# Chunk preparation in a fused attention block: token layout, order of the keys' turn, and who divides the entries' weights

## The chip, the core and the metric

One core of one Trainium2 chip. The metric is the device time of one launch in microseconds (us). The core's engines run side by side, each in the order of its own queue: TensorE (PE in the profile, its weight loads as PEld), VectorE (DVE), ScalarE (ACT), GpSimd (POOL), and SyncE (SP), which here issues nearly all DMAs, in order. Data meet between engines through semaphores.

## The reference

Four sequences of 1024 tokens, 512 features, 16 heads of 128. In short:

```python
xn = layernorm(x)
q  = rope(rmsnorm(xn @ Wq + bq, qn_w))                      # 16 heads
w  = softmax over each 4 tokens of (xn @ Wcmp + bcmp)
entries = sum over each 4 tokens of w * xn                  # 256 a sequence
ck = rope(rmsnorm(entries @ Wk + bk, kn_w), last position of the four)
cv = entries @ Wv + bv
sc = q . ck / sqrt(128), entries that end later masked; top 8 of them
ctx_sparse = softmax over the 8 chosen, times their cv
lk = rope(rmsnorm(xn @ Wlk + blk, kn_w)); lv = xn @ Wlv + blv
ctx_local  = softmax over the last 128 tokens and itself (q . lk / sqrt(128)) @ lv
attn = ((ctx_sparse + ctx_local) * 0.5) @ Wo + bo
ffn  = fp8(xn * scale) / scale  @  fp8(W2 * scale1) / scale1
out  = x + attn + ffn
```

## The kernel before

**Tiles and units.** The 4096 tokens are 32 chunks t of 128 tokens, eight a sequence; c = t mod 8. A unit is one chunk and two heads, so a chunk has eight units u = 0 to 7, and there are 256 units. All weights stay in SBUF. The main loop (L969) runs over a step s = 8t + u. It is a software pipeline written out by hand: step s does the scores, weighing and turning of unit s, the values of unit s - 1, the output of unit s - 2, the local values' projection of s + 1, the normalizing and rotating of the queries and keys of s + 2, and the projection of queries and keys of s + 3. The order of the calls in the loop's body is the order of instructions on every engine; no scheduler changes it.

**A unit on TensorE**, in its order: scores (L718, L725, L728), queries and keys (`queries`, L576, four 128x512 products), output (L921), local values (`values_of`, L682, four 128x256 products), values (`values`, L888). The fp32 products run as two matmuls each. `queries` and `values_of` have the turned tokens `xnT` (features on partitions) as the operand that is loaded as weights. `xnT` is a tile of 128 x 128 x 4: token, then block of 128 features, so `xnT[:, :, k]` steps by four floats. `xone` is a contiguous copy of block 0 with a row of ones in place of feature 0 (`put_ones`, L478 on ScalarE and L479 on GpSimd, at u = 3), which brings the biases in; it is made of `xnT`, which is fetched from DRAM at the end of u = 2 (`fetch_tokens`, L471, four DMAs).

**A unit on VectorE**: masks and row maxima of the window (L750), the entries' mask, their eight largest and their removal (L761 to L773); the normalizing of unit s + 2 (`normalize`, L604); `settle`: with ScalarE's exponentials (L775, L783) it drops the entries that were not chosen (L791), takes the reciprocals of both totals (L801) and divides the entries' weights (L803), while ScalarE divides the window's (`settle_window`, L811); the first half of the rotation (L327); `turn` (L829): 32x32 transposes of both heads' weights into `probB`.

**Turning through DRAM.** A full turn of 128 x 128 is done with VectorE's transposes within blocks of 32 and a write and a fetch that move the blocks. For the weights: one write `pr` (L837), four fetches `probT` (L871), which TensorE's `values` of the next step needs. For queries and keys of s + 2: the rest of the rotation (`end_rotation`, L329 and L330), `turn_keys` (L657 and L660, four writes `qk`, L665) and two fetches (`fetch_keys`, L675). On SP, in a step: `pr`, `qk`, `probT`, `qT` and `lkT`, with the preparation's DMAs between them. Chunk 0 and the last unit turn on TensorE (`turn_here`).

**Preparing a chunk** is a generator, `chunk_prep`, of which a step of the loop runs a piece or two: layer norm (L343 to L360, with a second mean by ScalarE's L352), the four tokens' softmax (L372 to L384, L399 to L401), the turning of the tokens within blocks (L392, into `xb`) and its write to DRAM (L397), the weighing (L403), the sum of each four (L411) and its write (L420). It starts at u = 7 and is driven by `steps()`, which runs twice a step: once after `turn`, once after `to_output`, both ahead of `end_rotation` and `turn_keys`. Chunks t + 4 are prepared in chunk t; in chunks 1 to 3 a second one (`extra`) goes along in u = 2 and 3. `chunk_entries` makes the compressed keys and values of a group of four chunks (PE L511, L541); `chunk_eight` makes the fp8 product (L558, in u = 5 and on; its additions on GpSimd), and its scratch tiles are the two buffers that `xb` uses too.

Of the kernel before, what the change touches and what calls it, by code (L numbers as in the profile page):

```python
# [38 lines left out]
def kernel(  # L39
# [299 lines left out]
    def chunk_prep(t):  # L339
# [6 lines left out]
        yield "A0"  # L346
        yield "B0"
# [11 lines left out]
        yield "A1"  # L359
        nc.vector.tensor_scalar(xt, xt, mean, r, ALU.subtract, ALU.mult)  # L360
        yield "B1"
        if not t:
            turn_tokens_here(xt)
            yield "T"
# [3 lines left out]
        xb = scratch(f"xb_{t}")  # L368
        log = work.tile([P, 1], F32, tag="log", name=f"log_{t}", bufs=1)
        row = work.tile([P, 2, BLK], F32, tag="row", name=f"row_{t}", bufs=1)  # L370
        red = work.tile([P, BLK // RATIO], F32, tag="red", name=f"red_{t}", bufs=1)
        nc.vector.scalar_tensor_tensor(  # L372
            xb, xt, 1.0, wcmp_sb, ALU.mult, ALU.mult, accum_out=log
        )
        nc.vector.tensor_scalar(row[:, 0, :], ones, log, bcmp_sb, ALU.mult, ALU.add)
# [9 lines left out]
        yield "A2"  # L385
        yield "B2"
        if not t:
            yield from add_tokens_here(row, red, xb, wide)
            return


        nc.vector.transpose(  # L392
            xb.rearrange("p (b j k) -> p b k j", b=NB, k=KK),
            xt.rearrange("p (k b i) -> p b k i", b=NB, k=KK),
        )
        tokens[t] = dram.tile([P, HID], F32, tag="xb", name=f"xb_dram_{t}", bufs=GC + 2)
        nc.sync.dma_start(tokens[t], xb)  # L397
        yield "A3"
# [3 lines left out]
        yield "B3"  # L402
        nc.vector.tensor_tensor(  # L403
            xt.rearrange("p (b j k) -> p b j k", b=NB, k=KK),
            xb.rearrange("p (b j k) -> p b j k", b=NB, k=KK),
            row[:, 1:2, :].unsqueeze(3).to_broadcast([P, NB, BLK, KK]),
            ALU.mult,
        )
        yield "A4"
        few = work.tile([P, P], F32, tag="few", name=f"few_{t}", bufs=1)  # L410
        nc.vector.tensor_reduce(  # L411
            few.rearrange("p (n k) -> p n k", k=KK),
            xt.rearrange("p (n r k) -> p n k r", r=RATIO, k=KK),
# [7 lines left out]
        yield "B4"  # L421

    def add_tokens_here(row, red, xb, wide):

        few = scratch("few_here")
        nc.gpsimd.memset(few, 0.0)
        fours = row[:, 1, :].rearrange("p (n r) -> p n r", r=RATIO)
        nc.vector.tensor_reduce(red, fours, AX.X, ALU.add)
        nc.vector.reciprocal(red, red)
        nc.vector.tensor_tensor(fours, fours, wide(red), ALU.mult)  # L430
        nc.vector.transpose(row[:, 0, :], row[:, 1, :])
        wp = pp("weights_here")
        nc.tensor.matmul(
            wp[:, 0:P], row[:, 0, 0:1].to_broadcast([P, P]), ident, start=True, stop=True
        )
        yield "W"
        nc.vector.tensor_tensor(
            xb.rearrange("p (s k) -> p s k", k=KK),
            chunks[0][0],
            wp[:, 0:P].unsqueeze(2).to_broadcast([P, P, KK]),  # L440
            ALU.mult,
        )
        nc.vector.tensor_reduce(
            few[:, 0 : NE * KK].rearrange("p (n k) -> p n k", k=KK),
            xb.rearrange("p (n r k) -> p n k r", r=RATIO, k=KK),
            AX.X,
            ALU.add,
        )
        few_here.append(few)
        few_here.append(dram.tile([P, P], F32, tag="few_here", name="few_dram", bufs=1))  # L450
        nc.sync.dma_start(few_here[1], few[:, 0 : NE * KK])
        yield "B4"
# [3 lines left out]
    def turn_tokens_here(xt):  # L456

        xp = pp("xp")
        for k in range(KK):
            nc.tensor.transpose(xp[:, ts(k, P)], xt[:, ts(k, P)], ident)  # L460
        xnT = work.tile([P, P, KK], F32, tag="xnT", name="xnT_0")
        nc.scalar.copy(
            xnT.rearrange("p s k -> p k s"), xp.rearrange("p (k s) -> p k s", k=KK)
        )
        chunks[0] = (xnT, None)

    def fetch_tokens(t):
        xnT = work.tile([P, P, KK], F32, tag="xnT", name=f"xnT_{t}")
        turned = tokens.pop(t).rearrange("(a i) (b x) -> b i a x", a=NB, b=NB)
        for b in range(NB):  # L470
            nc.sync.dma_start(  # L471
                xnT[ds(b * BLK, BLK)].rearrange("i (a j) k -> i a (j k)", a=NB), turned[b]
            )
        chunks[t] = (xnT, work.tile([P, P], F32, tag="xone", name=f"xone_{t}"))

    def put_ones(t):
        xnT, xone = chunks[t]
        nc.scalar.copy(xone, xnT[:, :, 0])  # L478
        nc.gpsimd.memset(xone[0:1], 1.0)  # L479

    def chunk_entries(g, n):
# [10 lines left out]
        else:  # L492
            few = scratch(f"fewT_{g}_{n}")
# [14 lines left out]
        yield "B4"  # L508
# [10 lines left out]
        kv = work.tile([P, 2, D], F32, tag="kv", name=f"kv_{g}_{n}", bufs=1)  # L519
# [26 lines left out]
    def chunk_eight(t):  # L546
# [4 lines left out]
        src = xnT.rearrange("p s k -> p (s k)")  # L551
# [3 lines left out]
        x8 = x8.rearrange("p (s k) -> p s k", k=KK)  # L555
        fp = pp(f"fp_{t}")
        for k in range(KK):
            nc.tensor.matmul(  # L558
                fp, x8[:, :, k], w2_sb[:, k, :], start=(k == 0), stop=(k == KK - 1)
            )  # L560
# [10 lines left out]
    def queries(n):  # L571
# [3 lines left out]
        for k in range(KK):  # L575
            nc.tensor.matmul(  # L576
                qp,
                xnT[:, :, k] if k or not t else xone,
# [98 lines left out]
    def values_of(n):  # L677
# [3 lines left out]
        for k in range(KK):  # L681
            nc.tensor.matmul(  # L682
                vp[:, 0:256],
                xnT[:, :, k],
# [101 lines left out]
    def settle(n):  # L786
# [15 lines left out]
        for h in range(2):  # L802
            nc.vector.tensor_scalar(  # L803
                probs[h][:, spa], probs[h][:, spa], tot[:, h, 1:2], None, ALU.mult
            )

    def settle_window(n):
        _, _, loc, _ = columns(n)
        tot = units[n].pop("tot")
        for h in range(2):  # L810
            nc.scalar.mul(probs[h][:, loc], probs[h][:, loc], tot[:, h, 0:1])  # L811
# [129 lines left out]
    def until(g, step):  # L941
        for at in g:
            if at == step:
                break
# [12 lines left out]

    ready = {-1: [0], 0: [1], 1: [2, 3], 2: [4, 5], 3: [6, 7]}
    ready.update({t: [t + GC] for t in range(GC, NT - GC)})
    made = {0: (0, 2), 1: (0, GC), 3: (1, GC)}  # L960
# [3 lines left out]
    until(first, "T")  # L964
    small_constants()
    masks()
    start = chunk_entries(0, 1)

    for s in range(-3, NN + 2):  # L969
        t, u = place(s)  # L970

        if u == 7 and t + 1 in ready:
            regular = chunk_prep(ready[t + 1][0])
            running.append(regular)
        if u == 3 and 0 <= t < NT:
            load_x(t, "sum")
        if u == 4 and t in made:
            running.append(chunk_entries(*made[t]))
# [11 lines left out]
        if s < 0:  # L990
            if s == -3:
                until(first, "B4")
# [4 lines left out]
        for_unit(s, (settle_window,))  # L997
        for_unit(s + 2, (go_on_rotating,))
        if by_dma(s):
            turn(s)  # L1000
        steps()
        if len(ready.get(t, ())) == 2 and u in (2, 3):
            if u == 2:
                extra = chunk_prep(ready[t][1])
            until(extra, "A0" if u == 2 else "A2")
            if u == 2:
                next(regular)
# [3 lines left out]
        if len(ready.get(t, ())) == 2 and u in (2, 3):  # L1011
            until(extra, "B1" if u == 2 else "B4")
        if len(ready.get(t, ())) == 2 and u == 1:
            next(regular)
        if u == 3 and 0 <= t < NT - 1:
            put_ones(t + 1)
        for_unit(s + 2, (end_rotation,))
        if s + 2 >= NU:
            for_unit(s + 2, (turn_keys,))
# [12 lines left out]
        if u == 1 and len(ready.get(t, ())) == 2:  # L1032
# [75 lines left out]
```

## Time and profile before

| what | us |
|---|---|
| three timed runs | 2717.34, 2717.20, 2714.86 |
| their median | 2717.2 |
| the profiled execution | 2725.9 |
| its span, first to last instruction | 2723.7 |
| TensorE busy in it | 2652.3 |
| VectorE, ScalarE, GpSimd busy | 2318.3, 1257.7, 799.1 |

Times of instructions come from the profiled execution, which took 8.7 us longer than the median. In a line of the timeline the columns are start, duration of the whole group, engine, line of the kernel, operation, out<-in, shapes and how many; in brackets the idle time before it and what ended it. Durations of neighbouring matmuls overlap, so what one costs is the distance from start to start. In a line of a tile, the three durations are the shortest, the median and the longest in ns, followed by the first and last start. A line of the stretches has the stretch, its length, and then for each engine its busy time and the number of instructions, TensorE's clock, the DMA engines' share and GB/s. The granted TensorE clock is 0.992 of full over the span.

### The profile page before, as it was taken

How to read it: one execution, taken by the hardware profiler on the slowest of the kernel's cores; microseconds unless marked ns; L12 is line 12 of the kernel's file. 1: busy time of each engine (PE TensorE's matmuls, PEld its weight loads, DVE VectorE, ACT ScalarE, POOL GpSimd, SP SyncE). 2: the span in 40 equal slices, each digit the busy share in tenths (PEclk: the TensorE clock that was granted, in tenths of full speed). 3: DMA queues.
4: the chain of work that ended last, by engine and by line, in shares of the span. 5: the costliest groups of instructions: out<-in, count | busy, mean ns of one | idle time of the engine just before them, and what ended most of it. 6: DMA issues, size and time to landing. Idle time of an engine off the chain costs nothing.

```text
span 2723.7 us, 46686 instructions
## 1 busy us (share of the span) xinstructions
PE 2652.3 (97%) x11802; PEld 2086.2 (77%) x11837; DVE 2318.3 (85%) x8884; ACT 1257.7 (46%) x5067; POOL 799.1 (29%) x1151
## 2 busy tenths in 40 slices
PE   8999999999999999999999999999999999999997
PEld 5777777777777777777777778777777777777776
DVE  7888888898888888888988888888988888888885
ACT  3444444444444444444444444444444444444443
POOL 4522332223332223232233322232323323222221
PEclk9999999999999999999999999999999999999998
DMA  8455455665545555566555555655665555566653
GB/s 257 120 142 150 132 149 167 171 165 153 154 135 158 151 157 149 161 166 169 160 145 139 155 151 154 170 159 157 168 164 146 150 141 147 151 161 165 162 153 107
DMA packets 667067, 422.85 MB, mean 155 GB/s; under 512 B 326528, under 2 KB 616112, under 8 KB 666800
## 3 DMA queue, kind: packets, MB, share of 16 engines
q1 hardware_dynamic: 666192, 419.46, 56.0%
q8 instruction: 97, 1.59, 0.3%
q14 instruction: 170, 1.39, 0.2%
q10 hardware_dynamic: 608, 0.41, 0.1%
HBM read 225.42 MB, written 194.25 MB: 154 GB/s over the span
## 4 chain that ended last, share of the span: by engine, by line
PE 76%; DVE 11%; DMA 5%; SPq 3%; ACT 3%; issue 2%; POOL 1%; DVEq 0%; ACTq 0%
PE qp L576 25%; PE vp L682 13%; PE cp L888 12%; PE op L921 12%; PE sc L728 5%; PE sc L725 4%; PE sc L718 3%; DMA probT<-pr 2%; SPq L665 1%; SPq L871 1%; ACT prob L775 1%; DVE probB L829 1%; DVE sc L750 1%; DVE taken L773 1%; PE fp L558 1%
## 5 line engine op out<-in xcount | busy, mean ns | idle before, releaser
L576 PE MATMUL qp<-wqk,xnT 128*128 128x512 f32 x1552 | 711.5, 595 | 3.5 <-DMA wqk<-in_L_attn_Wlk_dram 3.5
L576 PEld LDWEIGHTS qp<-wqk,xnT 128*128 128x128 f32 x1552 | 478.0, 309 | 221.4 <-issue 64.9
L775 ACT ACTIVATE prob<-sc,neg 128x256 f32<-128x256 f32 (+1 forms) x512 | 235.9, 461 | 879.2 <-DVE taken L773 861.1
L682 PEld LDWEIGHTS vp<-wlv,xnT 128*128 128x128 f32 x2048 | 517.8, 325 | 91.9 <-issue 56.2
L682 PE MATMUL vp<-wlv,xnT 128*128 128x256 f32 x2048 | 516.4, 395 | 0.1
L921 PE MATMUL op<-wo,cT 128*128 128x512 f32 x1024 | 481.6, 593 | 3.4 <-ACT cT L903 3.3
L325 POOL TENSOR_TENSOR rb<-th,cs 128x256 f32<-128x256 f32 x256 | 204.1, 797 | 949.7 <-DVE th L604 941.6
L750 DVE CUSTOM_DVE_ANT_0 sc<-sc,mask_b 128x256 f32<-128x256 f32 (+1 forms) x512 | 210.9, 412 | 180.8 <-PE sc L728 170.8
L811 ACT ACTIVATE prob<-prob,tot 128x256 f32<-128x256 f32 (+1 forms) x512 | 225.6, 488 | 300.3 <-DVE tot L801 297.6
L921 PEld LDWEIGHTS op<-wo,cT 128*128 128x128 f32 x1024 | 193.6, 190 | 206.8 <-issue 144.9
L888 PE MATMUL cp<-probT,lv 128*128 128x128 f32 x1920 | 307.0, 281 | 38.6 <-DMA probT<-pr 37.0
L888 PEld LDWEIGHTS cp<-probT,lv 128*128 128x128 f32 x1920 | 279.2, 197 | 55.8 <-issue 46.4
L311 ACT ACTIVATE junk<-qp 128x128 bf16<-128x128 f32 x1024 | 278.7, 272 | 30.6 <-PE qp L584 6.2
L604 DVE SCALAR_TENSOR_TENSOR th<-qp,r,norm_w 128x128 f32<-128x128 f32 x1024 | 286.2, 343 | 0.9 <-POOL r L306 0.9
L829 DVE STREAM_TRANSPOSE probB<-prob 128x512 f32<-128x512 f32 (+2 forms) x494 | 282.2, 609 | 0.1
L306 POOL TENSOR_TENSOR r<-r,nhalf 128x4 f32<-128x4 f32 x256 | 266.7, 1042 | 21.4
L305 POOL TENSOR_SCALAR r<-ss 128x4 f32<-128x4 f32 x256 | 61.6, 241 | 696.9 <-ACT junk L311 693.6
L791 DVE SCALAR_TENSOR_TENSOR prob<-taken,prob 128x128 f32<-128x128 bf16 (+7 forms) x512 | 182.8, 358 | 96.3 <-ACT prob L783 95.0
L888 PE MATMUL cp<-probT,cv 128*128 128x128 f32 x1536 | 259.9, 279 | 0.0
L576 PE MATMUL qp<-wqk,xone 128*128 128x512 f32 x496 | 258.5, 603 | 0.0
L728 PE MATMUL sc<-ckT,qT 128*128 128x96 f32 (+7 forms) x1024 | 228.2, 305 | 2.7 <-ACT ckT L543 2.7
L888 PEld LDWEIGHTS cp<-probT,cv 128*128 128x128 f32 x1536 | 217.3, 196 | 0.0
(143 smaller groups left out, 3844.9 us busy)
## 6 DMA issues: line engine op xcount, KB each, us to landing
pr<-probB SPq DMA_DIRECT2D x127, 512.0 KB, 3.3
probT<-pr SPq DMA_DIRECT2D x508, 128.0 KB, 3.0
qk<-thb SPq DMA_DIRECT2D x992, 64.0 KB, 1.8
pr<-probB SPq DMA_DIRECT2D x96, 384.0 KB, 2.3
probT<-pr SPq DMA_DIRECT2D x384, 96.0 KB, 2.5
qT<-qk SPq DMA_DIRECT2D x248, 128.0 KB, 2.9
lkT<-qk SPq DMA_DIRECT2D x248, 128.0 KB, 3.1
x_norm<-_attn_hidden_states_dram SPq DMA_DIRECT2D x32, 256.0 KB, 3.3
```

Source lines behind the costliest of these rows:

```text
L306: nc.gpsimd.tensor_tensor(r, r, nhalf[: ss.shape[0], 0:n], ALU.pow)
L311: nc.scalar.activation(junk[: src.shape[0]], src, AF.Square, accum_out=acc)
L576: nc.tensor.matmul(qp, xnT[:, :, k] if k or not t else xone, wqk_sb[u][:, k, :], start=(k == 0), stop=(t > 0 and k == KK - 1),)
L604: nc.vector.scalar_tensor_tensor(th[:, i, :], qp[:, ts(i, D)], r[:, i : i + 1], norm_w[:, i // 2, :], ALU.mult, ALU.mult,)
L682: nc.tensor.matmul(vp[:, 0:256], xnT[:, :, k], wlv_sb[u][:, k, :], start=(k == 0), stop=(k == KK - 1),)
L728: nc.tensor.matmul(sc[:, spa], q, ckT[:, 0:m], start=True, stop=True)
L750: nc.vector.tensor_tensor_reduce(sc[:, h, loc], sc[:, h, loc], mask_b[:, loc], -1.0, TAKEN, ALU.add, ALU.min, neg[h][0],)
L775: nc.scalar.activation(probs[h][:, loc], sc[:, h, loc], AF.Exp, bias=neg[h][0], scale=-1.0, accum_out=tot[:, h, 0:1],)
L811: nc.scalar.mul(probs[h][:, loc], probs[h][:, loc], tot[:, h, 0:1])
L829: nc.vector.transpose(pb[:, :, ds(h * g, g), :], prob[:, parts[0] * P : (parts[-1] + 1) * P].rearrange("p (g b i) -> p b g i", b=NB, i=BLK),)
L888: nc.tensor.matmul(blocks(cp[:, h, :]), v, probT[:, :, h * len(parts) + i - parts[0], :], start=(i == parts[0]), stop=(i == parts[-1]),)
L921: nc.tensor.matmul(op, cT[:, h, :], wo_sb[u][:, h, :], start=(u == 0 and h == 0), stop=(u == NU - 1 and h == 1),)
```

## The change

1. The turned tokens are laid out as 4 blocks x 128 tokens, so that `xnT[:, k, :]` is contiguous. VectorE's transpose writes runs of 32, the write to DRAM becomes four DMAs with runs of 32 floats, and the fetch takes whole rows of 512. The sum of fours reads contiguous fours and goes to the first quarter of `xb`. The scratch products of the logits, the entries' `fewT` and `kv` share one buffer.
2. `end_rotation` comes straight after the rotation's first half, and `turn_keys` straight after `turn`, both ahead of `steps()` and the preparation.
3. The preparation goes in named pieces at fixed places from u = 6 of the chunk before to u = 3, a second one from u = 2 to 5. `xone` is made at u = 4 instead of u = 3, in one buffer instead of two. Entries are begun (their loads) at the top of u = 4, and are made twice more, as `made` tells: of three chunks at t = 1 and t = 3.
4. ScalarE divides the entries' weights too, after the window's of the same head; VectorE no longer does.

```diff
@@ chunk_prep
-        yield "A0"
-        yield "B0"
+        yield "statistics"
...
+            xb = scratch(f"xb_{t}")
+            nc.vector.transpose(
+                xb.rearrange("p (b k j) -> p b k j", b=NB, k=KK),
+                xt.rearrange("p (k b i) -> p b k i", b=NB, k=KK),
+            )
+            tokens[t] = dram.tile(
+                [BLK, NB * KK, NB, BLK], F32, tag="xb", name=f"xb_dram_{t}", bufs=GC + 2
+            )
+            for a in range(NB):
+                nc.sync.dma_start(
+                    tokens[t].rearrange("i f a j -> a i f j")[a],
+                    xb[ds(a * BLK, BLK)].rearrange("i (f j) -> i f j", j=BLK),
+                )
...
+        yield "turned"
...
-            xb, xt, 1.0, wcmp_sb, ALU.mult, ALU.mult, accum_out=log
-        )
+            products, xt, 1.0, wcmp_sb, ALU.mult, ALU.mult, accum_out=log
+        )
+        yield "logits"
...
+        yield "exponentials"
...
-        nc.vector.transpose(
-            xb.rearrange("p (b j k) -> p b k j", b=NB, k=KK),
-            xt.rearrange("p (k b i) -> p b k i", b=NB, k=KK),
-        )
-        tokens[t] = dram.tile([P, HID], F32, tag="xb", name=f"xb_dram_{t}", bufs=GC + 2)
-        nc.sync.dma_start(tokens[t], xb)
...
-        few = work.tile([P, P], F32, tag="few", name=f"few_{t}", bufs=1)
+        few = xb[:, 0:P]
         nc.vector.tensor_reduce(
-            few.rearrange("p (n k) -> p n k", k=KK),
-            xt.rearrange("p (n r k) -> p n k r", r=RATIO, k=KK),
+            few.rearrange("p (b e k) -> p b k e", b=NB, k=KK),
+            xt.rearrange("p (b k e r) -> p b k e r", b=NB, k=KK, r=RATIO),
@@ fetch_tokens
-        xnT = work.tile([P, P, KK], F32, tag="xnT", name=f"xnT_{t}")
-        turned = tokens.pop(t).rearrange("(a i) (b x) -> b i a x", a=NB, b=NB)
+        xnT = work.tile([P, KK, P], F32, tag="xnT", name=f"xnT_{t}")
+        turned = tokens.pop(t).rearrange("i (b k) a j -> b i (k a j)", b=NB)
@@ put_ones
+        xone = work.tile([P, P], F32, tag="xone", name=f"xone_{t}", bufs=1)
@@ queries, values_of
-                xnT[:, :, k] if k or not t else xone,
+                xnT[:, k, :] if k or not t else xone,
...
-                xnT[:, :, k],
+                xnT[:, k, :],
@@ settle
-        for h in range(2):
-            nc.vector.tensor_scalar(
-                probs[h][:, spa], probs[h][:, spa], tot[:, h, 1:2], None, ALU.mult
-            )
-
-    def settle_window(n):
-        _, _, loc, _ = columns(n)
+
+    def divide(n):
+        _, _, loc, spa = columns(n)
         tot = units[n].pop("tot")
         for h in range(2):
-            nc.scalar.mul(probs[h][:, loc], probs[h][:, loc], tot[:, h, 0:1])
+            for part, cols in enumerate((loc, spa)):
+                nc.scalar.mul(probs[h][:, cols], probs[h][:, cols], tot[:, h, part : part + 1])
@@ the loop
+    FIRST_HALF = {6: "statistics", 7: "mean", 0: "logits", 1: "exponentials", 2: "weights", 3: "added"}
+    SECOND_HALF = {7: "turned", 2: "weighed"}
+    FIRST_HALF_MORE = {2: "statistics", 3: "normalized", 4: "weights", 5: "added"}
+    SECOND_HALF_MORE = {2: "mean", 3: "logits", 4: "weighed"}
...
-    made = {0: (0, 2), 1: (0, GC), 3: (1, GC)}
+    made = {0: (0, 2), 1: (0, 3), 2: (0, GC), 3: (1, 3), 4: (1, GC)}
...
         if u == 4 and t in made:
-            running.append(chunk_entries(*made[t]))
+            begun = chunk_entries(*made[t])
+            next(begun)
+        if u == 5 and t in made:
+            running.append(begun)
...
         for_unit(s, (settle,))
-        for_unit(s, (settle_window,))
-        for_unit(s + 2, (go_on_rotating,))
+        for_unit(s, (divide,))
+        for_unit(s + 2, (go_on_rotating,), (end_rotation,))
         if by_dma(s):
             turn(s)
+        if s + 2 >= NU:
+            for_unit(s + 2, (turn_keys,))
         steps()
...
+        host = t if u < 4 else t + 1
+        if host in ready:
+            until(regular, FIRST_HALF.get(u))
...
-        if u == 3 and 0 <= t < NT - 1:
+        if u == 4 and 0 <= t < NT - 1:
             put_ones(t + 1)
-        for_unit(s + 2, (end_rotation,))
-        if s + 2 >= NU:
-            for_unit(s + 2, (turn_keys,))
```

## The prediction

> **What bounds the kernel now.** I read the page first (busy shares, chain of work that ended last), then TensorE's waits, then the tiles that the change touches, then single units on the timeline. A unit is one pass of the loop: two heads of one 128-token chunk, eight units (u = 0 to 7) a chunk, 256 units. c is the chunk's place in its sequence.
>
> ```profile
> span 2723.7 us, 46686 instructions
> ...
> PE 2652.3 (97%) x11802; PEld 2086.2 (77%) x11837; DVE 2318.3 (85%) x8884; ACT 1257.7 (46%) x5067; POOL 799.1 (29%) x1151
> ...
> PE 76%; DVE 11%; DMA 5%; SPq 3%; ACT 3%; issue 2%; POOL 1%; DVEq 0%; ACTq 0%
> ```
>
> TensorE (PE) is busy 97% and is 76% of the chain, so 71.4 us are left in which it stands still, and apart from those the time is what its queue costs. VectorE (DVE) at 85% is next. TensorE's waits, in us in total, times, longest:
>
> ```profile
> PE cp L888 <- DMA probT<-pr: 37.0, 26, 4.0
> PE tp L852 <- ACT prob L811: 10.7, 4, 5.0
> ```
>
> 37.0 of the 71.4 us are waits for the turned probabilities, fetched from DRAM. By time, 5.9 of them lie in the last two units and 31 in chunks 1 to 30; these chunks have 39 us of TensorE waits in all (those over 0.15 us added up; the most of the rest are 4.1 for ckT and 2.8 for cT), the head and chunk 0 some 14, the tail 12. Two stretches of eight units, the second of the two without any preparation of a later chunk (columns: busy us of PE, its loads, VectorE, ScalarE, GpSimd):
>
> ```profile
> 1276.76:1364.50 87.74, 85.90 (x389) 68.00 (x389) 78.77 (x276) 39.93 (x156) 24.88 (x34) 1.00 0.59 160
> 2505.48:2590.14 84.66, 84.61 (x388) 67.64 (x389) 71.28 (x261) 38.95 (x153) 23.07 (x30) 1.00 0.59 159
> ```
>
> With preparation TensorE idles 1.8 us, without it nothing. So preparing chunks makes the waits, and the rest is matmul time.
>
> **Contiguous tokens: TensorE.** Weight loads and matmuls that read the turned tokens (min/median/max ns), and the load of the contiguous copy xone:
>
> ```profile
> L682 PEld LDWEIGHTS vp<-wlv,xnT x2048: 307/330/332, 27.3 to 2690.5; 128*128 128x128 f32 x187
> L682 PE MATMUL vp<-wlv,xnT x2048: 379/397/501, 27.5 to 2690.7; 128*128 128x256 f32 x187
> L576 PEld LDWEIGHTS qp<-wqk,xnT x1552: 307/308/333, 10.5 to 2668.3; 128*128 128x128 f32 x194
> ```
>
> ```profile
> L576 PEld LDWEIGHTS qp<-wqk,xone x496: 189/190/333, 88.8 to 2665.7; 128*128 128x128 f32 x166
> ```
>
> ```profile
> 1505.21 1.88 PE L921 MATMUL op<-wo,cT 128*128 128x512 f32 x4
> 1506.92 2.02 PE L682 MATMUL vp<-wlv,xnT 128*128 128x256 f32 x8
> 1508.78 0.61 PE L888 MATMUL cp<-probT,lv 128*128 128x128 f32 x4
> ```
>
> A load at a step of four floats takes 308 to 330 ns, a contiguous one 190. Under the 512-column matmuls this is hidden: four take 1506.92 - 1505.21 = 1.71 us, 428 ns each, with 190 ns loads, and the queries, with 308 ns loads, come at 428 ns too. The 256-column ones should take half, 214 ns, but eight take 1508.78 - 1506.92 = 1.86 us, 232 each. Contiguous loads therefore should give up to 8 x 18 = 0.15 us a unit; since some already run at the fastest duration I use mean 395 less min 379 over all 2048: **-32.8 us**. The bounds are 0 (the load is not what slows them) and 256 x 0.15 = 38. I take 32.8, because the contiguous loads of L888 keep up with 128-column matmuls at (0.61 - 0.28) / 3 = 0.11 us each.
>
> [...]
>
> The trace has 330 against 190 ns for the same 128 columns.
>
> **Added on TensorE.** Two more runs of the compressed entries, (0, 3) and (1, 3): eight matmuls of 232 ns and a transpose, 2.1 us each: **+4.2 us**. Nothing hides them.
>
> **VectorE.** A prepared chunk loses 1084 - 668 ns on the token transpose (L392 against the contiguous 128x512 ones of L829) and something of L411's 1063 (between none and 1063 - 652, the latter a plain pass of 512; I take 0.4): some 0.8 us a chunk. The sparse divide, 512 x 296 ns, goes to ScalarE. None of it is on TensorE's path; it buys room. But VectorE now waits for the divide before it turns the probabilities (queued behind: this transpose, the keys', the preparation, the next unit's weigh; the next waiting is SP with the write of pr). ScalarE does 256 + 192 columns twice, 0.44 and (estimated between the 0.30 and 0.44 of its neighbours) 0.37 us start to start, 1.6 us; VectorE meanwhile does the rotation (0.33 + 0.52) that is moved here and the first transpose. The second transpose ends about 0.3 us later than now at c = 6, 0.1 at c = 2.
>
> **Keys turned before the preparation.** Today, in a unit with preparation:
>
> ```profile
> 1987.11 0.34 SPq L837 DMA_DIRECT2D pr<-probB  x1
> 1989.32 0.36 SPq L931 DMA_DIRECT2D out_dram<-x_sum  x1
> 1990.53 2.61 SPq L665 DMA_DIRECT2D qk<-thb  x4
> 1993.25 1.83 SPq L871 DMA_DIRECT2D probT<-pr  x4
> ```
>
> SP is in order: the probT fetches stand behind the keys' four writes, and these wait until VectorE is through 1.6 us of preparation and x_sum's add. TensorE waited 1.71 us for this fetch at 1998.12. Afterwards the keys are turned 0.8 us after pr, so qk issues from 1987.9 and probT some 2.6 us earlier: this wait goes, and so do its like in u = 1 to 3. ScalarE's copy to xone, which today waits 33.8 us in all for the tokens' DMA and so delays cT, comes a unit later, and the 2.8 us of TensorE's waits for cT go as well.
>
> The entries' five loads now stand ahead of the unit's pr on SP, 2.2 us of issue. I set them to 0: SP is idle for over 4 us there (lkT issued by 2509.05, pr at 2513.43). Without that gap they would cost up to 2.2 us in twelve places. The tokens' fetch keeps its place and its four issues. The buffer that products, fewT and kv now share is taken at u = 0 and u = 4, after its last reader at u = 7 and u = 5: 0.
>
> **What is late next.** First, u = 7: the tokens' write becomes four DMAs instead of one, issued between the keys' writes and probT. In a unit without preparation at c = 6, probT's last issue starts at 2507.53 and TensorE gets to it at 2512.48; at 3.0 us to landing 1.95 us are spare. Four issues of 0.45 us, 0.3 for the divide, 0.15 for a faster TensorE and some 0.5 of traffic make 2.75: a wait of 0.8 us, less at c = 1 to 3 (2.5 us to landing). Over 31 chunks at 0.5 us: 15 us. How long 2048 pieces of 128 bytes take to write no row tells. Below: no delay (the fetches of 128-byte pieces, fewT<-pooled, land in 2.2 us, as the tokens' write does now). Above: the mean packet, 56.0% x 16 x 2723.7 us / 666192 = 36.6 ns, times 128 a DMA engine, 4.7 us. I stay by fewT.
>
> [...]
>
> Second, u = 5: xone is made one unit later, at u = 4, behind the four squares on ScalarE and behind the rstd on GpSimd, and the next unit's queries need it. At c = 2:
>
> ```profile
> 1506.55 0.18 DVE L801 RECIPROCAL tot<-tot 128x4 f32<-128x4 f32 x1
> ...
> 1506.83 0.91 ACT L811 ACTIVATE prob<-prob,tot 128x256 f32<-128x256 f32 x2 [0.91 <-DVE tot L801]
> ...
> 1509.55 1.01 POOL L306 TENSOR_TENSOR r<-r,nhalf 128x4 f32<-128x4 f32 x1
> ...
> 1511.47 1.08 PE L576 MATMUL qp<-wqk,xone 128*128 128x512 f32 x2
> ```
>
> Two more divides put the squares 0.55 us later, so rstd ends at 1511.1 and the 0.20 us memset at 1511.35; TensorE is there at 1511.47 - 0.12: no wait, and no room. At c = 7 weighing and divides are longer by more than the period is, and I get 0.95 us. Over eight chunks 2.5 us, over 31 **9.5 us**. All of TensorE's later work queues behind it.
>
> Chunk 0 and the head: two divides more before each tensor transpose (+0.3 us where TensorE waits), less preparation beside the weight folding; the tokens' write, moved a unit ahead, holds SP's weight loads some 4 us, which are needed 20 us later. I set it to 0, within 4 either way. Tail: +0.5.
>
> **The sum.** Matmul time -32.8 + 4.2 = -28.6. Waits of chunks 1 to 30: 39 now; 15 + 9.5 + 4 (entries, unchanged) afterwards: -10.5. Tail +0.5. In all -38.6. The profiled execution took 2725.9 us (span 2723.7 and 2.2 around it), so it would take 2687.3; the median of the three timed runs lies 8.7 lower: **2678 us**.
>
> **Rivals.**
> - All waits hide: the small pieces cost nothing and xone is in time, -24.5 more: 2654. For it: chunks without preparation wait for nothing. Against: both rooms worked out above are under 2 us.
> - The loads are not what slows the values' matmuls (nothing contiguous at 256 columns is in the trace): +32.8, 2711. The change would not do what its first words say. Against: 395 ns and 330 ns go together.
> - VectorE's wait for ScalarE and the full chain take the waits back: 20 us, 2698. For it: at c = 6 and 7 VectorE's busy time, 78.77 of 87.74 us, with its pauses is nearly TensorE's.
> - **Slower**: the small writes stand in the DMA engines ahead of probT at u = 7. At 4.7 us an engine, 2.8 are left when the last is issued, 2.3 more than I counted, 71 us over 31 chunks, of which some 7 fall into room left at c = 0 to 3: +64, 2742. It decides from 39 / 31 = 1.25 us a chunk more than I allow. For it: half the packets are small already and the engines are busy 56%. Against: fewT's 2.2 us.
>
> **Chances.** Forecast 0.45; all hidden 0.15; loads 0.08; waits taken back 0.16; slower 0.13; the rest, no change, 0.03. A measurement of this kernel tells about 0.2% (5.4 us) from no change. The loads' case ends near that line, so half of it counts as no change: faster 0.80, same 0.07, slower 0.13. The range goes from all hidden with 38 for the loads (2649) to the loads' case with its 4 us of the head (2715); it leaves out the slow case and a few.
>
> **What would show it.** Right: L682's loads at 190 and its matmuls at 379 ns; probT waits gone at u = 1 to 3 and left at u = 7; a new wait of qp for xone at u = 5, longest at c = 7. Wrong: matmuls still at 397 (step one); no waits left, or long probT waits at u = 7 with tokens' writes landing after 4 us (step two); VectorE waiting for ScalarE above 0.5 us a unit.

## The result and the profile after

The changed kernel took 2722.6 us (median of 20 runs, 2714.9 to 2730.5), the kernel before 2717.6 us (20 runs, 2714.3 to 2720.5). The ratio is 1.0016, 95% interval 1.0009 to 1.0023: no gain, and just measurably slower at most. The forecast was 2678. The profiled execution of the changed kernel took 2724.1 us, its span 2722.3, against 2725.9 and 2723.7 before, so the two profiles can be held side by side. They are not quite the medians: by the medians the changed kernel is 5.0 us slower, by the profiles 1.8 us faster, and what follows explains the profiles.

The page of the changed kernel (span, busy us and share of each engine, share of the chain that ended last):

```profile
span 2722.3 us, 46795 instructions
...
PE 2637.3 (97%) x11855; PEld 1796.1 (66%) x11855; DVE 2220.5 (82%) x8382; ACT 1397.7 (51%) x5587; POOL 795.2 (29%) x1159
...
PE 68%; DVE 13%; ACT 8%; DMA 4%; SPq 3%; issue 3%; POOL 2%; ACTq 0%; DVEq 0%; POOLq 0%
```

TensorE's busy time fell by 15.0 us and its idle time rose from 71.4 to 85.0. VectorE is 98 us lighter, yet the chain passes less through TensorE (68 for 76%) and more through ScalarE (8 for 3%). The values' loads and matmuls (ns shortest/median/longest):

```profile
L684 PEld LDWEIGHTS vp<-wlv,xnT x2048: 186/190/191, 28.6 to 2693.8; 128*128 128x128 f32 x187
L684 PE MATMUL vp<-wlv,xnT x2048: 378/379/390, 28.7 to 2694.0; 128*128 128x256 f32 x187
```

This is what was forecast, 190 and 379 ns for 330 and 397. Busy time of this group is 483.8 us for 516.4. So 32.6 us were gained here and lost again elsewhere. TensorE's waits say where (us in total, times, longest; L887, L851, L730 and L578 of this kernel stand at L888, L852, L728 and L576 in the kernel before):

```profile
PE cp L887 <- DMA probT<-pr: 30.1, 20, 3.6
PE sc L730 <- ACT ckT L545: 18.1, 10, 3.1
PE qp L578 <- POOL xone L481: 9.2, 12, 2.7
PE tp L851 <- ACT prob L810: 9.1, 3, 4.7
```

The sum for probT is little smaller than 37.0, but it is another wait. Before, the waits lay mostly at the values of units u = 1 to 3; of these 1.0 us is left. Now 17.5 us lie at u = 7 of chunks 4 to 26 (15 times; 1.7 of it is listed under "issue" and not under probT) and 10.1 at u = 3 of chunks 1 to 3: the units in which a chunk's tokens are written, the second in those chunks where two chunks are prepared. The ckT wait was 2.7 us before, at most 0.8 at a time. Here are SyncE's queue (SPq) and TensorE around one of the stalls at u = 7:

```profile
1133.84 0.34 SPq L836 DMA_DIRECT2D pr<-probB  x1
1134.49 2.86 SPq L667 DMA_DIRECT2D qk<-thb  x4
1137.44 2.57 SPq L374 DMA_DIRECT2D xb_dram<-xb  x4
1140.11 2.00 SPq L870 DMA_DIRECT2D probT<-pr  x4
```

```profile
1141.20 1.89 PE L684 MATMUL vp<-wlv,xnT 128*128 128x256 f32 x8
1145.03 0.68 PE L887 MATMUL cp<-probT,lv 128*128 128x128 f32 x4 [1.93 <-DMA probT<-pr]
```

The keys' writes now start 0.65 us after pr, as forecast, but the tokens' four writes hold SyncE for 2.57 us ahead of the probT fetch. All 124 of them:

```profile
L374 SPq DMA_DIRECT2D xb_dram<-xb x124: 549/626/1738, 33.2 to 2297.9; - x124
```

And what comes after such a stall, in three stretches of some 3.41 us (busy us of PE, its loads, VectorE, ScalarE, GpSimd, with their instructions, then TensorE's granted clock, the DMA share and GB/s):

```profile
1142.95:1146.36 3.41, 1.48 (x13) 1.36 (x13) 2.49 (x6) 1.20 (x8) 1.50 (x2) 1.00 1.15 280
1146.36:1149.78 3.42, 3.42 (x18) 3.42 (x17) 0.00 (x0) 1.00 (x3) 0.00 (x0) 0.50 0.52 154
1149.78:1153.19 3.41, 3.41 (x11) 1.74 (x11) 2.75 (x14) 0.00 (x0) 0.00 (x0) 1.00 0.77 147
```

The stall of 1.93 us is followed by 3.42 us at a granted clock of 0.50. In that stretch a pair of L720's matmuls takes 0.42 us from its start to the next pair's (at 1147.36), where it takes 0.24 at full clock (at 173.26). By an estimate, half the stretch, that is 1.7 us more of the same loss, and in the list of waits it is not seen at all. In the whole profile such half-clock time rose from 47.5 to 62.4 us (the last stretch of each runs on past the last instruction; within the spans it is 45.1 and 61.4).

### The profile page after: what moved, and what is told of

It is laid out like the page before. It is cut to its first block, busy times and chain, and to the rows that moved or that the text cites. A ratio compares the mean times of both kernels' runs of the same rounds, so it can differ in the third digit from the quotient of the medians.

```text
span 2722.3 us, 46795 instructions
## 1 busy us (share of the span) xinstructions
PE 2637.3 (97%) x11855; PEld 1796.1 (66%) x11855; DVE 2220.5 (82%) x8382; ACT 1397.7 (51%) x5587; POOL 795.2 (29%) x1159
## 2 busy tenths in 40 slices
DMA packets 719292, 423.33 MB, mean 156 GB/s; under 512 B 394496, under 2 KB 668336, under 8 KB 719024
## 4 chain that ended last, share of the span: by engine, by line
PE 68%; DVE 13%; ACT 8%; DMA 4%; SPq 3%; issue 3%; POOL 2%; ACTq 0%; DVEq 0%; POOLq 0%
PE qp L578 23%; PE op L920 11%; PE cp L887 11%; PE vp L684 11%; PE sc L730 4%; PE sc L727 3%; PE sc L720 3%; ACT prob L810 2%; ACT prob L777 2%; DMA probT<-pr 2%; DVE sc L752 2%; ACT junk L311 1%; DVE taken L775 1%; SPq L870 1%; ACT prob L785 1%
## 5 line engine op out<-in xcount | busy, mean ns | idle before, releaser
L578 PE MATMUL qp<-wqk,xnT 128*128 128x512 f32 x1552 | 720.4, 601 | 3.7 <-DMA wqk<-in_L_attn_Wlk_dram 3.7
L578 PEld LDWEIGHTS qp<-wqk,xnT 128*128 128x128 f32 x1552 | 300.0, 194 | 380.6 <-issue 379.4
L810 ACT ACTIVATE prob<-prob,tot 128x256 f32<-128x256 f32 (+7 forms) x1024 | 381.9, 443 | 298.4 <-DVE tot L803 298.4
L684 PEld LDWEIGHTS vp<-wlv,xnT 128*128 128x128 f32 x2048 | 389.4, 190 | 161.1 <-issue 116.0
L684 PE MATMUL vp<-wlv,xnT 128*128 128x256 f32 x2048 | 483.8, 379 | 0.0
L887 PE MATMUL cp<-probT,lv 128*128 128x128 f32 x1920 | 301.5, 277 | 32.3 <-DMA probT<-pr 30.1
L828 DVE STREAM_TRANSPOSE probB<-prob 128x512 f32<-128x512 f32 (+2 forms) x494 | 308.8, 630 | 12.4 <-ACT prob L810 1.2
L887 PEld LDWEIGHTS cp<-probT,lv 128*128 128x128 f32 x1920 | 273.7, 193 | 54.6 <-issue 42.9
L578 PE MATMUL qp<-wqk,xone 128*128 128x512 f32 x496 | 264.2, 615 | 9.8 <-POOL xone L481 9.2
L306 POOL TENSOR_TENSOR r<-r,nhalf 128x4 f32<-128x4 f32 x256 | 265.4, 1037 | 21.3
L887 PE MATMUL cp<-probT,cv 128*128 128x128 f32 x1536 | 257.8, 277 | 0.0
L730 PE MATMUL sc<-ckT,qT 128*128 128x96 f32 (+7 forms) x1024 | 229.5, 306 | 18.1 <-ACT ckT L545 18.1
L887 PEld LDWEIGHTS cp<-probT,cv 128*128 128x128 f32 x1536 | 215.1, 194 | 0.0
```

Source lines behind the costliest of these rows:

```text
L306: nc.gpsimd.tensor_tensor(r, r, nhalf[: ss.shape[0], 0:n], ALU.pow)
L578: nc.tensor.matmul(qp, xnT[:, k, :] if k or not t else xone, wqk_sb[u][:, k, :], start=(k == 0), stop=(t > 0 and k == KK - 1),)
L684: nc.tensor.matmul(vp[:, 0:256], xnT[:, k, :], wlv_sb[u][:, k, :], start=(k == 0), stop=(k == KK - 1),)
L730: nc.tensor.matmul(sc[:, spa], q, ckT[:, 0:m], start=True, stop=True)
L810: nc.scalar.mul(probs[h][:, cols], probs[h][:, cols], tot[:, h, part : part + 1])
L828: nc.vector.transpose(pb[:, :, ds(h * g, g), :], prob[:, parts[0] * P : (parts[-1] + 1) * P].rearrange("p (g b i) -> p b g i", b=NB, i=BLK),)
```

## The experiments

Theory A: the loads' gain is real, and it is given back by places in in-order queues: the tokens' writes ahead of probT on SyncE, the ckT copy and the ones behind other work on ScalarE and GpSimd, each wait made dearer by the clock. Rivals: B, the small pieces in the DMA engines; C, VectorE's chain or the divides on ScalarE; others where they are named. All kernels were timed beside the kernel before, and each ratio is against it. A difference to the changed kernel is one of medians from two such timings; in them the kernel before took 2717.3 to 2718.6 us.

**The layout alone.** The kernel before, with the contiguous tile, in two forms. First with one write of whole rows, which leaves out the regrouping of the four blocks of tokens (their order in the tile is not the reference's, the work of the engines is the same):

```diff
-                xnT[:, :, k],
+                xnT[:, k, :],
...
-            nc.sync.dma_start(
-                xnT[ds(b * BLK, BLK)].rearrange("i (a j) k -> i a (j k)", a=NB), turned[b]
-            )
+            nc.sync.dma_start(xnT[ds(b * BLK, BLK)], turned[b])
```

> The kernel before with the contiguous layout of the turned tokens alone, with its single write of 2 KB rows at its old place; as in the kernel with one write the regrouping of the four token blocks is left out. Nothing else of the change: keys turned where they were, preparation in its old stages, VectorE dividing the entries' weights. Theory A (the faster loads are worth their 32.6 us where no wait comes in their place): 24 to 36 us less than the kernel before, 2682 to 2694, with the 379 ns matmuls of vp and the 37.0 us of probT waits grown by less than 8. Rival C (VectorE's chain sets the pace there, so that a faster TensorE only waits longer): less than 12 us gained, 2705 to 2718, the waits for probT grown by 20 or more.

2689.2 us, ratio 0.9896 (0.9883 to 0.9910). Rival C falls: the gain of the loads reaches the end almost whole.

```profile
PE cp L884 <- DMA probT<-pr: 35.0, 26, 4.1
PE tp L848 <- ACT prob L807: 11.4, 4, 5.0
```

The waits are those of the kernel before. Then with the regrouping, in the true order of tokens, with the change's four writes at the old place of the one:

> The kernel before with the contiguous layout alone, with the change's four writes of 128-byte pieces at the old place of its single write (output in the reference's order). Theory A (each of the four issues takes 0.6 us of SyncE ahead of the fetch of probT): 15 to 45 us more than the 2689 of the same kernel with one write, 2704 to 2734, and probT waits of 50 to 80 us in place of 35.0. Rival F (the writes only hurt at u=7, where the change put them; at the old place they are covered): within 8 us of 2689.

2723.3 us, ratio 1.0021 (1.0012 to 1.0030): 34.1 us more than with one write, more than the whole gain.

```profile
PE cp L892 <- DMA probT<-pr: 55.5, 46, 5.6
```

So the writes are not dear at u = 7 only (F falls), but also at this second place ahead of a probT fetch; here the new waits lie at the values of u = 2 and u = 1.

**The keys ahead alone**, in the kernel before:

```diff
-        for_unit(s + 2, (go_on_rotating,))
+        for_unit(s + 2, (go_on_rotating,), (end_rotation,))
         if by_dma(s):
             turn(s)
+        if s + 2 >= NU:
+            for_unit(s + 2, (turn_keys,))
```

> The kernel before with the keys' turning alone moved ahead of the chunks' preparation (the rotation's end and the keys' transposes and DMA issues right behind the turning of the weights). Theory A (VectorE's order sets the probT waits at u=1 to u=3 only through the preparation that stands behind, not through the keys): small, minus 8 to plus 6 us against the kernel before, 2709 to 2724. Rival D (the keys moved ahead are themselves what costs: their four DMA issues now stand ahead of the fetch of probT on SyncE in every unit): slower by 8 to 25 us, with new waits for probT. The changed kernel shows 2.1 to 2.9 us for these issues where the kernel before shows 1.8.

2716.7 us, ratio 0.9995 (0.9986 to 1.0004). D falls, and the time is as A has it, but not for A's reason: the waits did change.

```profile
PE ep L511 <- DMA fewT<-pooled: 15.5, 8, 3.0
PE op L921 <- ACT cT L903: 11.8, 7, 2.4
PE cp L888 <- DMA probT<-pr: 11.3, 8, 3.2
```

The probT waits fell from 37.0 to 11.3 us; what came late instead is the preparation, whose sums TensorE now waits for at the entries. That keys ahead need a preparation that is begun earlier fits this, and fits the last kernels below, but was not run by itself.

**The tokens' writes**, in the changed kernel. The late write:

```diff
-            for a in range(NB):
-                nc.sync.dma_start(
...
+            unwritten.append((t, xb))
...
         if s + 2 >= NU:
             for_unit(s + 2, (fetch_keys,))
+        write_tokens()
```

> The changed kernel with the four DMA issues of a chunk's turned tokens kept back until after the fetch of the keys, so that on SyncE's queue they stand behind the fetch of probT instead of ahead of it. Theory A (the gain of the loads was given back to waits: the four issues take 2.6 us of SyncE at u=7, probT's fetch goes out late, TensorE waits at the product of values, and after each wait of about 2 us its granted clock is halved for some 3.4 us): the 30.1 us of waits of the context matmul for probT fall below 8, the half-clock time falls with them, 25 to 35 us less than the changed kernel, about 2690 to 2697. Rival B (not the issues, but the 2048 pieces of 128 bytes in the DMA engines delay probT): the pieces move later but still meet a transfer, the waits stay within 8 of 30.1, time within 6 us of the changed kernel. Rival C (TensorE waits for the VectorE chain, and SyncE is only the last to arrive): the waits change name, not size; time within 6 us.

2699.2 us, ratio 0.9938 (0.9926 to 0.9951), 23.4 less than the changed kernel, just short of the range of A.

```profile
PE qp L585 <- POOL xone L488: 20.9, 13, 6.2
PE sc L737 <- ACT ckT L552: 18.2, 10, 3.1
PE tp L858 <- ACT prob L817: 11.0, 4, 5.2
PE cp L894 <- DMA probT<-pr: 7.2, 6, 3.3
```

The waits for probT went. In chunks 1 to 3 the time was not kept: TensorE now waits there for the ones, 17.5 us at the next chunk's first queries where it was 6.0. The same writes issued by GpSimd (`nc.sync` to `nc.gpsimd` in that call, nothing else):

> The changed kernel with the four writes of the turned tokens issued by GpSimd in place of SyncE, at the same place of the program, with the same pieces of 128 bytes. Theory A (the time of SyncE's issues is what delays the fetch of probT): the probT waits at u=7 go as with the late write, to below 10 us, 12 to 25 us less than the changed kernel, 2698 to 2711; less of it if GpSimd's own issues delay the ones or the rotation. Rival B (the pieces in the DMA engines, ahead of probT's): the pieces still run at the same time, the waits stay above 25 us, time within 5 us of the changed kernel.

2697.9 us, ratio 0.9926 (0.9914 to 0.9939), probT waits 7.4 us. So these writes cost the probT fetch nothing once SyncE does not issue them. This run does not separate A from B, though: in its profile the pieces of 128 bytes are gone too. The packets under 512 bytes are 331008 where the changed kernel has 394496, fewer by 31 x 2048, and the writes stand on a queue of their own, half of whose packets are of 4096 bytes and half of 4:

```profile
q0 software_dynamic: 3968, 8.13, 1.1%
```

The changed kernel's own trace separates them. In chunks with c = 4 to 7, where the tokens' writes stand between, the last probT fetch is issued 6.98 us after pr (median of 12 units), elsewhere 4.18 us after it (115 units). From its issue to its landing it takes 3.21 and 3.11 us. So it is issued 2.8 us late, and the pieces ahead of it add 0.1 us: B falls by this. Last, whole rows from SyncE at the changed kernel's place, again without the regrouping, in one write and in four:

> The changed kernel with one write of whole 2 KB rows at the same place, and the reads as the kernel before has them (pieces of 512 bytes), into the contiguous tile; it leaves out the regrouping of the four blocks of tokens, so that their order in the tile is not the reference's, at the same work on every engine. Theory A (time of SyncE's issues): one issue of about 0.35 us in place of four of together 2.6 us, so about 2.2 us of lateness goes at each u=7: most of the 30.1 us of probT waits go, 18 to 32 us less than the changed kernel, 2691 to 2704. Rival B (pieces of 128 bytes in the engines): the same gain, but then the kernel with the late write gains nothing. Rival C (the VectorE chain): within 6 us.

> As the kernel with one write (whole 2 KB rows, regrouping left out), but in four writes of 32 rows at the same place. It tells the number of issues from the size of the pieces. Theory A with a price for each issue: four issues of about 0.4 us (the four of the keys took 1.8 us together), 1.3 us more than one write, so half of the probT waits are back: 6 to 14 us over the 2702 of the kernel with one write. Theory A with a price by pieces: an issue of 32 pieces is cheap, within 5 us of 2702. Rival B: within 5 us of 2702 as well, but then the writes by GpSimd gain nothing.

2702.0 (ratio 0.9944, 0.9932 to 0.9956) and 2702.4 us (0.9948, 0.9935 to 0.9961). The number of issues alone costs no time that can be told:

```profile
L372 SPq DMA_DIRECT2D xb_dram<-xb x124: 302/422/1579, 34.4 to 2281.2; - x124
```

An issue of 32 rows takes 0.42 us, one of 512 pieces 0.63. Four make 1.7 or 2.5 us, and the room before TensorE asks for probT, 1.95 us by the prediction's own reading, lies between; that this is why four issues of rows cost nothing is argued, not shown. In the profile of the four the probT waits are 16.8 us for 9.8, so the room is nearly used up.

**The ckT copy.** A dropped `yield "A7"` puts it right behind its transpose, ahead of the mean and the squares. In the changed kernel ScalarE is busy like this while TensorE waits 2.89 us for L545 at 738.48:

```profile
734.41 1.71 ACT L810 ACTIVATE prob<-prob,tot 128x256 f32<-128x256 f32 x4 [1.97 <-DVE tot L803]
736.02 0.71 ACT L351 ACTIVATE x_norm<-x_norm,off 128x512 f32<-128x512 f32 x1
...
736.73 0.25 ACT L311 ACTIVATE junk<-qp 128x128 bf16<-128x128 f32 x1
...
738.17 0.26 ACT L545 COPY ckT<-cp 128x128 f32<-128x128 f32 x1
```

Before, the divides of this unit took 0.91 us, and no mean stood between them and the squares:

```profile
735.52 0.91 ACT L811 ACTIVATE prob<-prob,tot 128x256 f32<-128x256 f32 x2 [1.97 <-DVE tot L801]
...
737.78 0.26 ACT L543 COPY ckT<-cp 128x128 f32<-128x128 f32 x1
```

The copy comes 3.76 us after the first divide's start instead of 2.26.

> The changed kernel with the copy of the entries' turned keys (ckT) put out right behind their transpose, one stage earlier in ScalarE's order, ahead of the mean's accumulation and the squares. Theory A (the copy is late because it stands behind what the change put ahead of it in ScalarE's queue): the 18.1 us of waits of the scores for ckT and the 1.9 us of the weights' transposes fall below 4, and the clock's halving behind the longest of them goes; 14 to 24 us less than the changed kernel, 2698 to 2708. Rival E (the copy is late because the entries' chain on VectorE and TensorE is late, whatever stands ahead on ScalarE): the waits stay within 5 of 18.1, time within 5 us.

2708.7 us, ratio 0.9967 (0.9955 to 0.9980), 13.9 less, just short of the range of A. The waits for ckT fell to 2.4 us (E falls), but those for probT rose:

```profile
PE cp L886 <- DMA probT<-pr: 41.7, 26, 3.2
```

TensorE comes to the values of u = 7 right after these scores, now up to 2.9 us earlier, and waits there instead.

**VectorE divides again** (the loop over `part` in `divide` cut to the window, and VectorE's `tensor_scalar` for the entries back):

> The changed kernel with VectorE dividing the entries' weights again, as the kernel before does; all else as changed. Theory A (the two more divides on ScalarE cost little of their own; the waits come from where the writes, the copy and the ones stand): within 8 us of the changed kernel, waits for ckT still above 12 and for probT above 25. Rival C (the divides on ScalarE are what made ckT, the ones and the weights late): the waits for ckT and the ones fall below 8 together, 15 to 30 us less than the changed kernel, 2692 to 2708.

2727.9 us, ratio 1.0035 (1.0021 to 1.0048), 5.3 more, at the edge of what can be told, with 15.4 us of waits for ckT and 39.0 for probT. The divides on ScalarE are no loss (a gain of 7.7 us in the kernel with all three places, below), and only a small part of ckT's lateness.

**The ones.** ScalarE's copy and GpSimd's row ahead of the preparation at u = 4:

```diff
+        if u == 4 and 0 <= t < NT - 1:
+            put_ones(t + 1)
         for_unit(s + 2, (go_on_rotating,), (end_rotation,))
```

(and the two lines gone from behind it). Alone, and then the other two without it:

> The changed kernel with the ones alone moved ahead of the chunks' preparation at u=4. Theory A (each wait has its own place and price): the 9.2 us of waits of the queries for the ones go, 5 to 12 us less than the changed kernel, 2710 to 2717. Rival H (TensorE's waits stand in series: a wait removed uncovers the next one in the same chunk): the waits for the ones go, but those for probT and ckT grow by about as much, within 4 us of the changed kernel.

> The changed kernel with the late write and the early ckT copy, the ones where the change put them. Theory A (the gains add): 23 and 14 us, 2685, and the ones are then worth some 22 us, since their waits grew to 20.9 us once the write was late. Rival H (in series): more than the sum, 2672 to 2680, because each of the two alone had its gain eaten by the other's wait (probT's waits rose from 30.1 to 41.7 us when ckT was early), and the ones are worth 10 to 15.

2715.8 us alone (0.9994, 0.9985 to 1.0003), 6.8 less than the changed kernel; its 9.2 us of waits went, and ckT's rose to 23.9. The time is as A has it, the growth elsewhere as H has it in part. The late write with the early copy: 2677.7 us (0.9856, 0.9842 to 0.9869), 44.9 less, where the two alone add up to 37.3. That is H's range: the waits stand in series, and each of the three repairs alone has the waits of another grow (the ones' from 9.2 to 20.9 us, probT's from 30.1 to 41.7, ckT's from 18.1 to 23.9).

**All three places.**

> The changed kernel with three places moved: the tokens' writes behind the fetch of the keys, the ckT copy right behind its transpose, and the ones (ScalarE's copy and GpSimd's row) ahead of the chunks' preparation at u=4 in place of behind it. Theory A (the waits are independent, each from a place in an in-order queue): the gains add, 23 from the writes, 14 to 24 from ckT, and 15 to 25 from the ones, whose wait had grown to 20.9 in the kernel with the late write: 2650 to 2675, and the half-clock time below that of the kernel before. Rival C (the chain of VectorE sets the pace and the next wait takes their place): 2690 to 2700, with new waits of the same sum elsewhere.

2662.6 us, ratio **0.9796** (0.9782 to 0.9809): 60.0 less than the changed kernel and 55 less than the one before.

```profile
PE tp L857 <- ACT prob L816: 9.7, 4, 4.7
PE cp L893 <- DMA probT<-pr: 8.5, 12, 2.3
PE cp L893 <- ACT cv L532: 5.5, 2, 2.8
PE sc L736 <- ACT ckT L551: 4.4, 5, 1.8
```

Half-clock time is 33.0 us. The singles add up to 44.1 (23.4, 13.9, 6.8), so 16 us come only together. Two parts of the change were then undone in this kernel:

> The kernel with the three places moved (2662.6), with the keys' turning put back behind the chunks' preparation, as the kernel before has it. Theory A (the keys ahead are what took away the probT waits of u=1 to u=3, 13 us at u=2 of chunks 8 to 27 and 20 us at u=3 of chunks 1 to 3 in the unit table): 10 to 30 us more than 2662.6, 2673 to 2693, with probT waits of 20 to 40 us. Rival G (the spreading over ten units is enough for that, the keys ahead are idle): within 6 us of 2662.6.

> The kernel with the three places moved (2662.6), with VectorE dividing the entries' weights again. In the changed kernel the same undoing cost 5 us. Theory A (VectorE's 65 us of work are off the path in most units, but late in those that host a chunk's preparation): 3 to 12 us more than 2662.6. Rival C (the divides on ScalarE hold up what stands behind them there): 3 or more us less.

With the keys behind the preparation 2716.6 us (0.9992, 0.9983 to 1.0001): 54.1 us more. The sign was A's, the size nearly twice what was expected. With VectorE dividing, 2670.2 us (0.9824, 0.9811 to 0.9838): 7.7 more. The first, on SyncE and TensorE:

```profile
1131.39 0.34 SPq L842 DMA_DIRECT2D pr<-probB  x1
1134.14 1.78 SPq L673 DMA_DIRECT2D qk<-thb  x4
1136.04 1.82 SPq L876 DMA_DIRECT2D probT<-pr  x4
```

```profile
PE cp L893 <- DMA probT<-pr: 51.2, 50, 4.3
```

The keys' writes go out 2.75 us after pr instead of 0.65, and the fetch behind them as late. With the preparation spread over ten units that happens in all of them, 50 waits for 26.

## Why the prediction was wrong

| term of the sum (us of the profile) | predicted | measured |
|---|---|---|
| contiguous loads | -32.8 | -32.6 |
| two more runs of the entries | +4.2 | +3.9 |
| old probT waits of chunks 1 to 30 | -31 | -31, with 1.0 left |
| probT behind the tokens' writes | +15 | +27.6 |
| the ones at u = 5 | +9.5 | +9.2 |
| ckT, against 4.1 before | 0 | +15.9 |
| cT | -2.8 | -1.9 |
| half clock, half of 62.4 - 47.5 (an estimate) | not counted | +7.4 |

The measured column adds up to -1.5 where the spans differ by -1.4. That is closer than it deserves: the tail, with some 6 us less in the last chunk, and small waits are not in it, the estimate for half clock counts stretches in which TensorE stands still too (6.7 us before, 5.1 in the changed kernel), and TensorE's busy time fell by 15.0 where the three terms that lie on it give 21.3.

- **Loads, keys, entries:** right in mechanism and size. For the loads the trace of the kernel before had 330 against 190 ns for the same 128 columns, the changed kernel has 190, and the layout alone, 28 us faster, shows that the gain reaches the time. The keys' step is also shown the other way round, by the 54 us that it costs to take it back. For **xone** the wait came where it was forecast in the unit, but its size is in part luck: 9.5 us were spread over 31 chunks, longest at c = 7 (0.95 us), and 6.0 of the 9.2 lie in chunks 1 to 3 (up to 2.7 us), where two chunks are prepared; at c = 7 it is 0.42.
- **The step that failed first** is "Four issues of 0.45 us ... Over 31 chunks at 0.5 us: 15 us". The mechanism and the place were named, and 15 became 27.6. Most of the lack is the second preparation of chunks 1 to 3, whose writes fall at u = 3 and were not counted there: 10.1 us in three stalls. The rest is at u = 7, 17.5 us: 0.45 us is about what an issue of the probT fetches or of the keys' writes takes (medians 0.43 and 0.45 us in the changed kernel), and one of 512 pieces takes 0.63 us. The question that was argued at length, how long the pieces take in the DMA engines, was the wrong one: behind them the fetch lands 3.21 us after its issue instead of 3.11. The slower rival (2742) falls with that; the estimate behind it took 36.6 ns a packet, and packets of 128 bytes took 11 ns (median in the changed kernel's trace).
- **"4 (entries, unchanged)"** is the second, and the larger error in the sum: the added divides were weighed for the probabilities and for the ones, but neither they nor the mean, now at u = 7, for the third thing that waits in ScalarE's queue, the ckT copy. Its waits measured 20.0 us (18.1 for the scores, 1.9 for a transpose), and moving it gave 13.9 us.
- **The clock** was not in the sum. It adds some 7.4 us net, by the estimate above.
- **The rival "waits taken back"** came true in its direction only: 20 us was its price, 37 were lost, and not through VectorE waiting for the divide. VectorE waits for that 1.2 us in the whole run, and taking the divide back made the kernel no faster. The loads' rival fell at once with 379 ns.

What stays open: how ckT's lateness divides between the mean, the divides and a TensorE that arrives earlier. Taking the divides away left 15.4 of the 18.1 us; the mean was not moved alone.

## What to carry to other kernels

For each instruction that a change adds or moves, list everything that stands behind it on its in-order engine and ask when each is due, and give a DMA issue the price of its own pattern: the same bytes took 0.34 us to issue as one write, 1.7 as four of whole rows and 2.5 as four in short runs. Give a place to what is due first (here the probT fetch, the ckT copy, the ones) ahead of work that is needed a chunk later. Test repairs together as well as alone, since waits that stand in series hide each other: 44 us by single repairs, 60 by all three.

## What the runs showed of the hardware

**The granted clock, in windows of 3.41 us.** In every profile here the half-clock stretches last 3.41 us or twice that (but for the one in which the profile ends) and begin on one grid of 3.41 us from start to end of the run. For the first ten profiles I added up TensorE's idle time in each grid window that itself had the full clock, from 100 us after the start to 60 us before the end. All 50 windows with 1.95 us or more idle were followed by half clock; of 20 with 1.7 to 1.95 us it was 8; of 7302 below 1.7 us none. In the six profiles taken afterwards, 30 of 30 windows above 1.9 us were followed by half clock, and none of 4376 below. The last 60 us, not in these counts, are less clean: 42 of 45 windows above 1.9 us were followed by half clock, and three, with 1.91, 1.97 and 2.00 us, were not. A stall's price went with where it fell. A stall of 3.33 us at 171.9 us of the changed kernel was cut by the grid into 1.63 and 1.70 and cost no clock, while one of 1.93 us inside a window cost the 1.7 us estimated above.

The changed kernel's runs spread over 15.7 us, those of the kernel before over 6.2 (20 runs each), those with all three places over 4.3 (4 runs only). What makes the first of these wider was not tested.

**An issue's time goes with its pattern.** On SyncE 0.34 us for a write of 128 rows of 2 KB in the kernel before, 0.42 for 32 such rows, 0.63 for 512 pieces of 128 bytes (medians). GpSimd took 0.69 us for the last, which there went out in packets of 4096 bytes.

```profile
L374 POOL DMA_DIRECT2D xb_dram<-xb x124: 652/692/866, 33.0 to 2268.6; - x124
```
